# A graph-attention and graph-convolution kernel with a planned step order: a new plan with bends per stage, seven early x tiles in y's ring, and four row tables

## The chip, the cores and the metric

The kernel runs on one core of one Trainium2 chip; the other cores are idle. The metric is the device time of one execution in microseconds (us), the median of several runs. Everything is in float32, except for two scratch tiles.

## The reference, cut to what matters

`x` is (32, 512, 1024): 32 batches b, 512 channels c, 1024 nodes n. `adj` is (512, 512).

```python
# layer 0: attention over nodes, then a projection by adj
h = relu(layernorm(x, axis=-1))              # mean and variance over the 1024 nodes
q = einsum('c,bcn->bn', wq, h)
k = einsum('c,bcn->bn', wk, h)
s = q[:, None, :] + k[:, :, None]            # (b, m, n)
s = where(s > 0, s, 0.01 * s)
att = softmax(s, axis=-1)
agg = einsum('bcn,bmn->bcm', h, att)
x = x + relu(einsum('oc,bcm->bom', adj, agg) + bm[None, :, None])
# layer 1: a projection by adj * adj, elementwise
h = relu(layernorm(x, axis=-1))
x = x + (einsum('bnf,nm->bmf', h, adj * adj) + bias)
```

The score of a pair of nodes depends on q[n] + k[m] alone, and the leaky relu has two branches. For a fixed m the nodes n with q[n] above -k[m] take one branch and all others the second. If the nodes are sorted by q, each m needs one sum over the nodes that come before some position and one over those that come after it. So the attention needs no 1024 x 1024 matrix: it needs the rank of each q, running sums of weighted rows in sorted order from both sides, and for each m a look-up at one position.

## The kernel before

**Work of a batch.** Each batch passes through these stages; names are those of the functions, with their lines in the profile.

- `load` (L223) brings four x tiles of 128 channels x 1024 nodes (512 KB each) by SyncE's queue into a ring `xp` of 7 buffers. `stats`, `norm`, `slopes`, `relu` (L234 to L253) make the layer norm: two statistics instructions a tile and small ones on VectorE, the square root (L244) and the relu (L257) on ScalarE. In layer 0 the relu writes over the x tile.
- `scores` (L265): 32 small matmuls on PE (L269) give q and k as rows; a copy on ScalarE and a round trip over DRAM spread q to all partitions (`qrow`, 512 KB). `columns` (L280) transposes them into columns, two PE instructions (L283). `factors` (L293) makes small vectors on VectorE and ScalarE.
- `value` (L369), eight times: four matmuls each (L372) project 128 nodes by adj; `spread` (L377) copies the result out of PSUM on ScalarE.
- `rank` (L304), eight times on VectorE: how many q are below each node's. `lower` (L323), eight times on ScalarE: how many q lie below -k. `to_rows` (L341), `from_rows` (L353) turn counts into row numbers.
- `scatter` (L382), eight times on GpSimd: an indirect DMA writes the projected rows, with q as a last column, in sorted order into a table in DRAM, `td`. There are three tables, taken in turn by batch. `fetch` (L396) reads them back in sorted order by SyncE's queue, as nine blocks of 126 rows.
- `weights`, `later`, `totals`, `stationary` (L406 to L441) make the exponential weights and masks for the running sums.
- `scan` (L452), nine times on PE: two pairs of matmuls (L455) make the running sums of a block, upward in one half of the partitions, downward in the other. `sums` (L461) follows each scan on ScalarE: it copies the last row of either half into the next block (L465, L466), and then the whole result (L468, L469), which goes to the table by two DMAs. So a scan needs the two row copies of the scan before.
- `gather` (L474), eight times on GpSimd: an indirect DMA fetches for each m the two sums and the row at its position. `excess` and `divide` (L483, L490) make the three factors of the softmax; `weigh` (L500, ScalarE) and `combine` (L504, VectorE, two per 128 nodes) add the three rows by them.
- `turn` (L510), eight times: four transposes on PE (L513) bring 512 nodes x 128 channels back to channel-major form; VectorE adds the relu to the residual (L515), which is x again, brought by `reload` (L229) into a ring `yp` of 7 buffers, since the relu wrote over the first copy.
- Layer 1: the same layer norm on y (the relu writes into a ring of four h tiles), `lift` (L262) adds the bias on VectorE, `propagate` (L517), eight times four matmuls (L520), and `finish` (L526) on VectorE, after which the row of tiles goes out.

**Order of the work.** The order is written out by a plan, not by loops. `PLAN` gives each stage a time for each of its pieces, in us from the batch's start. Batch b starts at b x T, with T = 79.96 (L541). `plan` (L534) hands each piece to `at` (L212), which adds the batch's start and, at the two ends of the program, a bend: `LAST` (last three batches) subtracts a curve of the time in the batch, `FIRST_SHIFT` (first five) adds one. All steps of all batches are then sorted by this time (L566) and emitted in that order; each engine and each queue works through its own instructions in the order of emission. So the times only sort. An engine that reaches an instruction early waits for it, and all that stands behind it on that engine waits too.

A batch of the plan spans some 470 us from its first load to its last finish, so about six batches are in progress at a time: in one period PE does scores, columns and values of batch b, scans of b - 1, turns and propagates of two earlier ones.

**Buffers.** PSUM has eight banks in one ring, used by all PE stages. The tile pools set how far stages may run ahead: `v` (8), fetched blocks (5 of three), sums (2), one gathered tile `G` of eight times 128 rows, small tiles mostly 2, `B` 4, `idg` and `arg` 3. Only one x tile of the program, the fourth of batch 1, is loaded into y's ring (L224). Before the first batch, ScalarE's queue writes four pads into each of the three tables (L189, L190), and PE transposes adj into `wmT` (L192).

Of the kernel before, what the change touches and what calls it, by code (L numbers as in the profile page):

```python
# [24 lines left out]
FAR = -1.0e30  # L25
PLAN = {
    "columns": (5.64,),
    "combine": (
        219.19, 223.04, 210.22, 211.36, 209.63, 210.28, 206.38, 209.6, 225.53,
        228.03, 220.14, 223.34, 225.03, 228.74, 208.88, 211.99,  # L30
    ),
    "divide": (201.44,),
    "excess": (197.53,),
    "factors": (34.87,),
    "fetch": (74.37,),
    "finish": (276.66, 282.71, 287, 301.14, 329.23, 329.75, 319.26, 338.77),
    "from_rows": (70.69,),
    "gather": (166.9, 167.4, 174.29, 175.46, 169.28, 190.2, 170.94, 177.02),
    "later": (84.78,),
    "lift": (257.62, 269.93, 271.07, 272.69),  # L40
    "load": (-128.41, -79.79, -90.39, -54.69),
    "lower": (22.54, 28.23, 27.44, 32.99, 8.04, 17.98, 32.02, 49.72),
    "norm0": (-13.33,),
    "norm1": (246.23,),
    "propagate": (267.02, 272.05, 280.31, 288.2, 304.83, 309.75, 312.6, 314.28),
    "rank": (13.66, 14.97, 27.68, 11.26, 36.34, 41.76, 32.23, 38.44),
    "reload": (211.38, 199.1, 198.01, 219.5),
    "relu0": (-9.09, -8.28, -8.01, -5.63),
    "relu1": (255.11, 255.75, 257.61, 257.81),
    "scan": (90.8, 98.9, 110.43, 116.3, 124.4, 137.24, 146.6, 154.57, 156.26),  # L50
    "scatter": (42.7, 37.63, 33.89, 33.08, 60.84, 49.95, 55.02, 49.29),
    "scores": (3.58,),
    "slopes0": (-13.06,),
    "slopes1": (249.1,),
    "spread": (28.19, 22.49, 20.23, 15.13, 33.75, 48.49, 42.32, 30.04),
    "stationary": (87.74, 100.59, 124.44),
    "stats0": (-88.94, -73.62, -80.02, -31.03),
    "stats1": (236.05, 245.64, 244.58, 238.48),
    "sums": (91.04, 103.93, 115.73, 121.32, 128.67, 145.61, 149.72, 155.13, 157.36),
    "to_rows": (29.48, 45.73),  # L60
    "totals": (89.71,),
    "turn": (230.81, 230.13, 230.45, 232.2, 233.84, 234.71, 233.3, 233.76),
    "value": (6.29, 12.68, 8.15, 4.57, 19.9, 20.34, 17.49, 19.32),
    "weigh": (212.94, 205.72, 204.24, 202.28, 221.56, 216.76, 220.58, 203.48),
    "weights": (84.77,),
}
LAST = (0.94, 0.36, 0.02,)
LAST_KNOTS = (60, 95, 130, 150, 215, 250, 275, 300, 345, 400)
LAST_GAIN = (0, 1.2, 5.7, 20.4, 20.4, 46.5, 53, 74.2, 87.6, 87.6)
FIRST_KNOTS = (-60, 60, 150, 250, 350)  # L70
FIRST_SHIFT = (
    (1.7, -1.4, -0.5, -1.8, -0.5),
    (-1.2, -1.1, -0.4, 0.7, -0.3),
    (-1.7, -1.1, -0.5, 5.2, -0.3),
    (-1.6, -1.2, 3.8, -1.4, -1),
    (1.8, 0.9, 1.3, 0.6, 0.5),
)
# [4 lines left out]
def kernel(  # L82
# [99 lines left out]
    tds = [dr.tile([6 * NB * HP, W], F32, name=f"td_{i}") for i in range(3)]  # L182
# [23 lines left out]
    def bend(knots, values, t):  # L206
        t = min(max(t, knots[0]), knots[-1])
        for a, b, u, v in zip(knots, knots[1:], values, values[1:]):
            if t <= b:
                return u + (t - a) * (v - u) / (b - a)  # L210

    def at(s, t, f, *args):  # L212
        time = s.t0 + t
        if B - 1 - s.b < len(LAST):
            time -= LAST[B - 1 - s.b] * bend(LAST_KNOTS, LAST_GAIN, t)
        if s.b < len(FIRST_SHIFT):
            time += bend(FIRST_KNOTS, FIRST_SHIFT[s.b], t)
        steps.append((time, len(steps), f, args))
# [378 lines left out]
```

## Time and profile before

| | us |
|---|---|
| median of 3 runs | 2414.36 (2412.83 to 2418.43) |
| the profiled execution | 2416.79 |
| its span, from first to last instruction | 2415.1 |
| busy PE in the first 240 us | 191.4 |
| busy PE from 240 to 2240 (2000 us) | 1998.1 |
| busy PE from 2240 to the end (175.1 us) | 154.0 |

The profile is of one execution. Busy time is what the instructions of an engine cover; PE is TensorE's matmuls, DVE VectorE, ACT ScalarE, POOL GpSimd, SP SyncE, and a "q" behind the name is that engine's queue of DMA issues. A group's row gives the line, the engine, the operation, what it writes and reads, and how often. In a timeline each row is a start, a duration, and the instructions run together; brackets show the idle time of the engine just before and what ended it. The chain of waits follows the work that ended last back in time: at each step to what released it, or to the instruction before it on its engine. PE's ends are modelled, so a PE that is shown busy may also be waiting inside an instruction: a matmul that takes longer than its kind usually does is a sign of that. PEclk is the granted clock as a share of the full one.

### The profile page before, as it was taken

The numbers are of one execution on the slowest core, as the hardware profiler recorded it, in microseconds if no ns is written. First come the engines' busy times: TensorE is split into PE (matmuls) and PEld (weight loads), VectorE is DVE, ScalarE is ACT, GpSimd is POOL, SyncE is SP. The second block draws the span as 40 slices with busy tenths as digits, with TensorE's granted clock in tenths as the row PEclk, the third lists the DMA queues.
The fourth block names the chain that finished last, engine by engine and source line by source line (L and its number), as shares of the span: only waits on it lengthen the run. The fifth ranks groups of instructions, "written<-read, shape, count | busy, mean of one in ns | idle before, by whom it ended". The sixth has DMA issues, their size and how long they took to land.

```text
span 2415.1 us, 28224 instructions
## 1 busy us (share of the span) xinstructions
PE 2343.5 (97%) x7632; PEld 986.1 (41%) x7632; DVE 1932.3 (80%) x5012; ACT 1591.2 (66%) x2879; POOL 704.7 (29%) x973
## 2 busy tenths in 40 slices
PE   6889999999999999999999999999999999999898
PEld 2233444443444443444443444443444444444333
DVE  6568787888788888787888888888888888887766
ACT  3667667777676677676777676677666677666541
POOL 2233232233232223232233232223232223232310
PEclk8889999999999999999999999999999999999999
DMA  4698988898898898898898898898898898898772
GB/s 157 164 286 284 279 289 260 268 298 284 275 289 265 255 295 281 273 291 259 253 299 284 278 290 263 254 293 287 273 281 273 251 293 289 273 284 256 237 284 99
DMA packets 206522, 642.87 MB, mean 266 GB/s; under 512 B 29030, under 2 KB 29158, under 8 KB 206364
## 3 DMA queue, kind: packets, MB, share of 16 engines
q1 hardware_dynamic: 146704, 370.65, 54.6%
q0 software_dynamic: 57344, 268.99, 29.3%
q10 hardware_dynamic: 2316, 1.43, 0.3%
q8 instruction: 62, 1.02, 0.2%
q14 instruction: 96, 0.79, 0.1%
HBM read 429.94 MB, written 211.02 MB: 265 GB/s over the span
## 4 chain that ended last, share of the span: by engine, by line
PE 92%; ACT 2%; DMA 2%; DVE 1%; issue 1%; POOL 0%; SPq 0%; ACTq 0%; POOLq 0%; DVEq 0%
PE pv L372 37%; PE pg L520 35%; PE sc L455 13%; PE tr L513 4%; PE pq L269 2%; DMA vs<-td 1%; ACT vs L465 1%; DMA g<-td,idg 1%; ACT x L257 1%; ACT g L502 0%; DVE y L515 0%; DMA td<-pad 0%; PE pd L434 0%; PE pr L283 0%; DMA bm_sb<-in_L_gnn_bm_dram 0%
## 5 line engine op out<-in xcount | busy, mean ns | idle before, releaser
L520 PE MATMUL pg<-h,wsq 128*128 128x512 f32 x2048 | 937.1, 602 | 0.8 <-ACT h L257 0.8
L372 PE MATMUL pv<-wmT,x 128*128 128x512 f32 x2048 | 912.0, 599 | 0.0
L520 PEld LDWEIGHTS pg<-h,wsq 128*128 128x128 f32 x2048 | 373.7, 191 | 515.0 <-issue 476.1
L372 PEld LDWEIGHTS pv<-wmT,x 128*128 128x128 f32 x2048 | 380.8, 191 | 494.8 <-issue 450.7
L477 POOL DMA_INDIRECT g<-td,idg x256 | 246.2, 962 | 800.1 <-DVE qk L288 204.0
L385 POOL DMA_INDIRECT td<-v,idx x256 | 286.7, 1120 | 571.2 <-ACT g L502 186.5
L465 ACT COPY vs<-sc 1x512 f32<-1x512 f32 x256 | 145.7, 569 | 418.1 <-PE sc L455 417.8
L325 ACT ACTIVATE junk<-qrow,qk 128x1024 bf16<-128x1024 f32 x256 | 294.6, 1151 | 141.9 <-DMA qrow<-qd 140.9
L455 PE MATMUL sc<-vs,sm 128*64 128x512 f32 x1152 | 344.0, 631 | 29.7 <-ACT vs L465 20.3
L506 DVE SCALAR_TENSOR_TENSOR g<-g,cf 128x512 f32<-128x512 f32 x512 | 350.0, 747 | 24.8 <-ACT g L502 24.5
L515 DVE SCALAR_TENSOR_TENSOR y<-tr,nbm,y 128x512 f32<-128x512 f32 x256 | 178.8, 744 | 109.2 <-PE tr L513 109.2
L528 DVE SCALAR_TENSOR_TENSOR y<-pg,bm_sb,y 128x512 f32<-128x512 f32 x256 | 188.2, 739 | 85.0 <-PE pg L520 85.0
L468 ACT COPY t<-sc 128x512 f32<-128x512 f32 x288 | 168.6, 585 | 32.4 <-PE sc L455 23.4
L314 DVE TENSOR_SCALAR_CACHE_REDUCE junk<-qrow,qk,cnt 128x640 bf16<-128x640 f32 (+6 forms) x224 | 180.5, 806 | 8.2
L309 DVE TENSOR_SCALAR_CACHE_REDUCE junk<-qrow,qk 128x384 bf16<-128x384 f32 (+6 forms) x224 | 165.9, 740 | 9.3 <-DMA qrow<-qd 7.9
L502 ACT ACTIVATE g<-g,cf 128x512 f32<-128x512 f32 x256 | 163.9, 715 | 2.6 <-DVE cf L496 2.6
L239 DVE BATCH_NORM_STATS2 st<-x 128x6 f32<-128x512 f32 x256 | 162.0, 674 | 2.7 <-DMA x<-in_x_dram 2.6
L239 DVE BATCH_NORM_STATS2 st<-y 128x6 f32<-128x512 f32 x256 | 160.6, 669 | 0.0
L455 PEld LDWEIGHTS sc<-vs,sm 128*64 128x64 f32 x1152 | 67.1, 137 | 228.4 <-issue 121.6
L263 DVE TENSOR_TENSOR y<-y,bias_sb 128x1024 f32<-128x1024 f32 x128 | 153.4, 1220 | 4.5 <-ACT h L257 4.5
L466 ACT COPY vs<-sc 1x512 f32<-1x512 f32 x256 | 147.7, 577 | 5.5
L257 ACT ACTIVATE h<-y,nmr,rstd 128x1024 f32<-128x1024 f32 x128 | 149.2, 1237 | 2.9 <-PE pg L520 2.3
(107 smaller groups left out, 1827.8 us busy)
## 6 DMA issues: line engine op xcount, KB each, us to landing
vs<-td SPq DMA_DIRECT2D x192, 384.8 KB
td<-t SPq DMA_DIRECT2D x576, 128.2 KB
x<-in_x_dram SPq DMA_DIRECT2D x128, 512.0 KB
y<-in_x_dram SPq DMA_DIRECT2D x128, 512.0 KB
out_dram<-y SPq DMA_DIRECT2D x128, 512.0 KB
qrow<-qd SPq DMA_DIRECT2D x32, 512.0 KB
td<-v,idx POOLq DMA_INDIRECT x256, 6.6
g<-td,idg POOLq DMA_INDIRECT x256, 10.7
```

Source lines behind the costliest of these rows:

```text
L239: nc.vector.bn_stats(st[:, i, :], s.x[c][:, ts(i, HALF)])
L257: nc.scalar.activation(h, s.x[c], AF.Relu, bias=s.nmr[:, c : c + 1], scale=s.rstd[:, c : c + 1])
L314: nc.vector.tensor_scalar(junk[:, j * P :], s.qrow[:, j * P :], qc, first, ALU.is_lt, ALU.add, accum_out=s.cnt[:, 1, j : j + 1],)
L325: nc.scalar.activation(junk, s.qrow, AF.Sign, bias=s.qk[:, 1, j : j + 1], accum_out=s.sgn[:, j : j + 1])
L372: nc.tensor.matmul(pv, s.h[c][:, ts(j, P)], wmT[:, c, :], start=(c == 0), stop=(c == NC - 1))
L385: i = nc.gpsimd.indirect_dma_start(tds[s.b % 3][:, :], bass.IndirectOffsetOnAxis(ap=s.idx[j // 4][:, j % 4 : j % 4 + 1], axis=0), v[:, :], ...
L455: nc.tensor.matmul(p[ts(k, HP), :], s.sm[i][k], s.vs[h][:, 0:C], start=True, stop=True)
L477: nc.gpsimd.indirect_dma_start(s.g[:, j, :], None, tds[s.b % 3][0 : 3 * NB * HP, :].rearrange("(s k) w -> s (k w)", k=3), bass.IndirectOff ...
L506: nc.vector.scalar_tensor_tensor(r, s.g[:, j, k * W : k * W + C], s.cf[:, k, j : j + 1], r, ALU.mult, ALU.add)
L515: nc.vector.scalar_tensor_tensor(xh, pt, nbm[:, o : o + 1], xh, ALU.max, ALU.add)
L520: nc.tensor.matmul(pg, wsq[:, r, ts(c, P)], s.h[r][:, ts(i, HALF)], start=(r == 0), stop=(r == NC - 1),)
L528: nc.vector.scalar_tensor_tensor(xh, s.pg.pop((c, i)), bm_sb[:, c : c + 1], xh, ALU.add, ALU.add)
```

## The change

1. Seven x tiles, all four of batch 1 and the first three of batch 2, are loaded into y's ring; before it was the fourth of batch 1 alone.
2. Four tables `td` in place of three; each has its four pad writes.
3. `nq` has three buffers in place of two, `B` five for four, `idg` and `arg` four for three.
4. `PLAN` has new times for all stages, and T is 79.84. `turn` is two stages, one for each half of the nodes, with four times each; the eight pieces are the same.
5. The curves for the first and last batches are gone. In their place each stage has a shift and a stretch (about the stage's mean time) for each of the first five batches, `FIRST`, and of the last five, `LAST`, of which the first pair belongs to the last batch.

No instruction of a batch is added or taken away; the order of the steps differs throughout. Cut to the stages that are spoken of below:

```diff
+TABLES = 4
 PLAN = {
-    "columns": (5.64,),
+    "columns": (1.84,),
-    "divide": (201.44,),
-    "excess": (197.53,),
+    "divide": (197.69,),
+    "excess": (192.58,),
-    "finish": (276.66, 282.71, 287, 301.14, 329.23, 329.75, 319.26, 338.77),
+    "finish": (275.07, 275.57, 281.48, 295.03, 317.93, 325.21, 315.57, 329.77),
-    "lower": (22.54, 28.23, 27.44, 32.99, 8.04, 17.98, 32.02, 49.72),
-    "norm0": (-13.33,),
+    "lower": (19.51, 17.67, 17.14, 24.76, 5.02, 13.05, 20.96, 48.33),
+    "norm0": (-19.68,),
-    "propagate": (267.02, 272.05, 280.31, 288.2, 304.83, 309.75, 312.6, 314.28),
-    "rank": (13.66, 14.97, 27.68, 11.26, 36.34, 41.76, 32.23, 38.44),
+    "propagate": (259.13, 265.4, 277.44, 283.36, 299.38, 300.5, 305.97, 309.52),
+    "rank": (10.11, 17.8, 19.14, 5.65, 29.55, 35.11, 29.97, 33.03),
-    "relu0": (-9.09, -8.28, -8.01, -5.63),
-    "relu1": (255.11, 255.75, 257.61, 257.81),
-    "scan": (90.8, 98.9, 110.43, 116.3, 124.4, 137.24, 146.6, 154.57, 156.26),
+    "relu0": (-13.28, -12.83, -12.78, -11.68),
+    "relu1": (248.39, 248.69, 248.95, 251.18),
+    "scan": (86.07, 89.94, 103.3, 112.5, 121.08, 133.74, 140.67, 149.41, 151.56),
-    "scores": (3.58,),
+    "scores": (-3.28,),
-    "sums": (91.04, 103.93, 115.73, 121.32, 128.67, 145.61, 149.72, 155.13, 157.36),
+    "sums": (86.61, 100.16, 109.91, 113.65, 123.33, 138.82, 142.68, 150.09, 152.34),
-    "turn": (230.81, 230.13, 230.45, 232.2, 233.84, 234.71, 233.3, 233.76),
-    "value": (6.29, 12.68, 8.15, 4.57, 19.9, 20.34, 17.49, 19.32),
-    "weigh": (212.94, 205.72, 204.24, 202.28, 221.56, 216.76, 220.58, 203.48),
+    "turn0": (224.81, 225, 224.25, 224.65),
+    "turn1": (229.2, 229.61, 229.06, 228.65),
+    "value": (1.31, 6.43, 2.58, -2.04, 12.64, 17.61, 9.29, 13.53),
+    "weigh": (211.43, 203.12, 199.8, 199.59, 214.55, 207.84, 213.35, 199.85),
...
 }
-LAST = (0.94, 0.36, 0.02,)
-LAST_KNOTS = (60, 95, 130, 150, 215, 250, 275, 300, 345, 400)
-LAST_GAIN = (0, 1.2, 5.7, 20.4, 20.4, 46.5, 53, 74.2, 87.6, 87.6)
-FIRST_KNOTS = (-60, 60, 150, 250, 350)
-FIRST_SHIFT = (
...
-)
+FIRST = {
+    "columns": ((10.25, 0), (-8.88, 0), (-1.28, 0), (-0.35, 0), (-4.55, 0)),
...
+    "norm0": ((-0.28, 0), (-7, 0), (-16.93, 0), (-5.48, 0), (-7.56, 0)),
...
+    "scan": ((-3.08, 0.008), (0.76, 0.008), (0.29, 0.01), (4.39, 0.049), (0.02, 0.004)),
...
+    "value": ((12.84, -0.049), (-4.18, -0.108), (-0.34, -0.035), (-1.68, 0.56), (-0.83, -0.076)),
...
+}
+LAST = {
...
+    "excess": ((-15.23, 0), (-5.2, 0), (-2.78, 0), (5.24, 0), (-2.45, 0)),
+    "finish": ((37.02, -0.24), (-20.28, -0.179), (-0.12, 0.054), (7.26, 0), (7.17, 0.076)),
...
+    "scan": ((-10.15, -0.309), (-4.12, -0.13), (1, -0), (0.78, -0), (-0.72, 0)),
...
+    "sums": ((-11.31, -0.321), (-3.79, -0.122), (0.67, -0.005), (1.54, -0.003), (-0.48, 0)),
...
+}
@@
-    tds = [dr.tile([6 * NB * HP, W], F32, name=f"td_{i}") for i in range(3)]
+    tds = [dr.tile([6 * NB * HP, W], F32, name=f"td_{i}") for i in range(TABLES)]
@@
-    def at(s, t, f, *args):
-        time = s.t0 + t
-        if B - 1 - s.b < len(LAST):
-            time -= LAST[B - 1 - s.b] * bend(LAST_KNOTS, LAST_GAIN, t)
-        if s.b < len(FIRST_SHIFT):
-            time += bend(FIRST_KNOTS, FIRST_SHIFT[s.b], t)
-        steps.append((time, len(steps), f, args))
@@
-        pool, tag = (yp, "y") if (s.b, c) == (1, NC - 1) else (xp, "x")
+        pool, tag = (yp, "y") if NC <= s.b * NC + c < NC + 7 else (xp, "x")
@@
-        s.nq = sp.tile([P, 2], F32, tag="nq", name=f"nq_{s.b}")
+        s.nq = sp.tile([P, 2], F32, tag="nq", name=f"nq_{s.b}", bufs=3)
...
-        s.B = sp.tile([P, NN], F32, tag="B", name=f"B_{s.b}", bufs=4)
+        s.B = sp.tile([P, NN], F32, tag="B", name=f"B_{s.b}", bufs=5)
@@
-        s.idg = sp.tile([P, NN], U32, tag="idg", name=f"idg_{s.b}", bufs=3)
+        s.idg = sp.tile([P, NN], U32, tag="idg", name=f"idg_{s.b}", bufs=4)
...
-        s.arg = sp.tile([P, 2, NN], F32, tag="arg", name=f"arg_{s.b}", bufs=3)
+        s.arg = sp.tile([P, 2, NN], F32, tag="arg", name=f"arg_{s.b}", bufs=4)
@@
+    T = 79.84
+
     def plan(s, f, name, *lead, args=None):
-        for n, t in enumerate(PLAN[name]):
-            at(s, t, f, s, *lead, *(args[n] if args else (n,)))
-
-    T = 79.96
+        times = PLAN[name]
+        mean = sum(times) / len(times)
+        shift, stretch = 0, 0
+        if s.b < len(FIRST[name]):
+            shift, stretch = FIRST[name][s.b]
+        elif B - 1 - s.b < len(LAST[name]):
+            shift, stretch = LAST[name][B - 1 - s.b]
+        for n, t in enumerate(times):
+            t = s.b * T + t + shift + stretch * (t - mean)
+            steps.append((t, len(steps), f, (s, *lead, *(args[n] if args else (n,)))))
@@
-        plan(s, turn, "turn", args=pairs_of(NH, range(NC)))
+        for i in range(NH):
+            plan(s, turn, f"turn{i}", i)
```

The other uses of `tds[s.b % 3]` become `tds[s.b % TABLES]`, and `pairs_of` is named `all_of`.

## The prediction, made before the changed kernel was run

> **What bounds the kernel now.** First the page: busy time by engine, and the granted TensorE clock over the span.
>
> ```profile
> span 2415.1 us, 28224 instructions
> PE 2343.5 (97%) x7632; PEld 986.1 (41%) x7632; DVE 1932.3 (80%) x5012; ACT 1591.2 (66%) x2879; POOL 704.7 (29%) x973
> PEclk8889999999999999999999999999999999999999
> ```
>
> TensorE sets the time, with two soft ends: the first 240 us hold 191 us of busy PE at a reduced clock, the stretch from 2240 on 154 of 175. I price the three parts apart. For the middle I read the busy times of two batches, each from one start of scores on PE to the next: batch 15, and batch 7 (columns: length; busy PE, its weight loads, VectorE, ScalarE, GpSimd; granted clock, DMA share, GB/s).
>
> ```profile
> 1052.54:1124.86 72.32, 72.23 (x240) 30.41 (x239) 60.21 (x157) 49.60 (x90) 21.97 (x30) 1.00 0.86 277
> 474.76:546.28 71.52, 71.52 (x239) 30.17 (x238) 62.85 (x163) 49.72 (x90) 21.84 (x30) 1.00 0.91 281
> ```
>
> The same 36 PE steps, PE busy throughout at full clock, yet 0.80 us apart. In the PE timeline, 22 batches in a row (8 to 29) take 72.32, batch 7 71.52. The chain of waits shows why: the end of batch 15, then that of batch 7.
>
> ```profile
> 1118.13 3.44 PE pg L520 x8
> 1121.57 1.03 PE sc L455 x4
> 1122.60 0.02 issue
> 1122.63 0.58 ACT vs L465
> 1123.21 0.04 issue
> 1123.25 1.67 PE sc L455 x4
> 1124.93 1.86 PE pq L269 x32
> ```
>
> ```profile
> 540.31 1.01 PE sc L455 x4
> 541.32 0.59 PE tr L513 x4
> 541.91 3.44 PE pg L520 x8
> 545.35 1.01 PE sc L455 x4
> 546.35 1.86 PE pq L269 x32
> ```
>
> In batch 15, scan 7 and scan 8 have one turn between them. Scan 8 needs two rows that sums 7 copies on ScalarE (L465, L466; 0.58 each): its first half starts late, and it takes 1.67 instead of 1.01, waiting for the second row. In batch 7 turn 5 and propagate 7 lie between, and both waits are gone: (1123.25 + 1.67) - 1121.57 = 3.35 for scan, turn, scan, against 1.01 + 0.59 + 1.01 = 2.61 and small switches, 0.80 in all by the period.
>
> Last the two ends, in the timelines of ScalarE and PE.
>
> ```profile
> 20.57 0.89 ACTq L189 DMA_DIRECT2D td<-pad  x2
> 21.49 1.28 ACT L244 ACT_TABLE_LOAD   x1 [21.49 <-DMA td<-pad]
> ...
> 2306.04 0.21 ACT L488 ACTIVATE cf<-cf 128x8 f32<-128x8 f32 x1 [5.74 <-DVE cf L487]
> ```
>
> ```profile
> 2306.81 2.30 PE L455 MATMUL sc<-vs,sm 128*64 128x512 f32 x4 [2.77 <-issue]
> 2365.29 5.39 PE L513 MATMUL tr<-ident,g 128*128 128x128 f32 x32 [3.60 <-DVE g L506]
> ```
>
> At the start the first norm stands behind the pad writes on ScalarE's queue. At the end ScalarE sits 5.74 in the excess of batch 30, which waits for the gather; sums 2 of batch 31 is queued behind it, and scan 3 waits 2.77.
>
> **What the Trainium skill says.** "Perfetto Trace Analysis", Identifying the Most-Contended Engine: TensorE's busy share is a poor measure, since matmuls are pipelined. The trace agrees: 72.23 of 72.32 busy hides 0.80 of waiting. Its Optimization Strategy names bubbles that repeat as a sign of missing memory; here one repeats 22 times and the cause is a copy, not a buffer. "TensorE: Matmul & The Clock Gate", Part 1: an idle PE falls back to half clock; the trace agrees (a scan takes 2.57 at 116.27, 1.01 in the middle). The same part says ScalarE and VectorE are strict first-in first-out, as the 5.74 shows.
>
> **The change, part by part.** I sorted both plans by their times and read the order on each engine.
>
> *Middle.* Every batch has the same PE steps. New: the second value stands before columns; turns go 2, 3, 0, 1, 7, 6, 4; and the end is scan 7, turn 5, propagate 7, scan 8: batch 7's order. One turn between scans 7 and 8 remains in batches 6 and 28 only, 22 before (7 to 28). Two turns (scan 8 at 1.32, so 0.3 lost) stand in three early batches before (2, 3, 5), in one after (4). Gain: (22 - 2) x 0.80 + 2 x 0.3 = 16.6. The cover is propagate 7 (3.44) and the turn (0.59) against 1.2 of copies, once ScalarE is free: scan 7 now comes 3.4 us earlier, but the four relus before sums 7 end at 1114.5 and scan 7 would end at 1119.1. Columns 3.5 later: VectorE waits, but the ranks it feeds start after qrow and totals anyway (14.0 us into the batch). T = 79.84 for 79.96 costs nothing: it only sorts.
>
> New queueing: divide now stands behind rank 5 and finish 1, 1.9 + 0.7 = 2.5 us, so it ends near 1095.0 instead of 1092.5. Weigh waits for it, and sums 4 and 5 queue behind weigh on ScalarE. Weigh started at 1096.41, when ScalarE came free: 1.4 to spare. Sums 5's copies end at 1105.9, scan 6 starts at 1106.9: 1.0 more. That covers the 2.5 but for 0.1, so I take 0; it costs something only where divide ends well after 1095.0 (rival below).
>
> *Front.* A fourth table adds four pad writes on ScalarE. Twelve take 13.05 to 23.72, 0.28 to 0.61 each with waits for landings up to 5.01. Four issues are 1.8; lower bound 0 (behind the relus), upper 1.8 + 5.0 = 6.8; I take 2.5, since the norm waits behind them. Seven x tiles in y's ring: SyncE no longer stops at 32 us for a slot until 56.5, so batch 2 is in SBUF early; but VectorE waited for x only 0.17 there, so 0, and up to 1.9 from the qrow of batch 1 no longer queued behind a 512 KB load. Their slots are free again when value of batches 1 and 2 ends, before the reloads at 162 and on. Norm and relu of batch 1 before the last lower (1.35): PE's 5.10 idle before scores 1 shrinks by 3, but the fetch of batch 0 lands at 79.8 as before; what stays is one more value put into that wait, 2.5. The seven bare scans of batch 0, each waiting for sums, stay (102.8 to 125.1). In batch 1 a value of batch 3 fills the wait between scans 7 and 8, and relus run earlier: 3.5 by scores 3, including the 2.5. Front: +2.5 - 3.5 = -1.0, bounds -6 and +5.
>
> *Tail.* Excess 30 moves behind sums 3 of batch 31: 2.77 of waiting and 2.4 of slow clock around scan 3 go (scan 2.30 for 1.01, propagate 4.67 for 3.63), but all eight weighs (5.0) then stand ahead of sums 5, a new wait of 1.5 at scan 6. Scan 8, and with it the last gather, come 3.7 to 4 earlier. From there on the chain is fixed by gather, combine, turn, stats, relu (2332.82 to 2381.76); propagate 5 of batch 30 moves into the 3.60 wait, but two finishes (1.4) now stand before the last slopes. I take -4.0, bounds -8 and +2. The finish 31 pushed late changes no order that matters: nothing follows it but itself.
>
> Spare copies of nq, B, idg, arg: no instruction, 0.
>
> Sum against the profiled execution: 2415.1 - 16.6 - 1.0 - 4.0 = 2393.5 span, 2395 with the 1.7 around it (2416.79). The three runs have a median of 2414.36, 2.4 below that execution, so 2414.4 - 21.6 = 2393.
>
> **Rivals.**
> *The ends gain more than I see* (shifts fitted per stage; 49 us of idle PE in the first 240, 21 at the end): front -6 or beyond and tail -8: about 2380. For: half of the bare scans' time is waiting. Against: the scans of the first two batches still stand bare in the new order.
> *The wait only moves.* PSUM or the copies hold scan 8 elsewhere: propagates 4, 5, 7 keep three banks to the next batch, scan 7 takes its bank 3.4 us earlier, before turns 7, 6, 4 are read. Half of the 0.80 back: 2401. All of it, or the order not realised: 2409 to 2414, no difference.
> *Slower: divide too late.* VectorE is 84% busy at 71.5 (60.2). Of the spare 1.4 + 1.0 = 2.4 the 2.5 has used all; what divide is late beyond 1095.0 is PE time in each of some 20 batches. From 1.1 us on that eats the gain of 21.6, and at 1.5 it costs 30 - 21.6 = 8: 2422. Against: in batch 7 VectorE did 62.9 within 71.52 unharmed.
>
> **How the numbers follow.** Middle gain as worked, ends within their bounds 0.66; ends gain more 0.08; half moved 0.08; no difference 0.06; slower 0.12. I call 0.2% (4.8 us) what a measurement can tell from none. Faster 0.82, same 0.06, slower 0.12. Likeliest 2393, its own range 2384 to 2402 (front and tail bounds, partly opposed). For 8 in 10 I cut the slower tail and the far end of the first rival: 2381 to 2411.
>
> **What would show it.** Right: starts of scores 71.5 apart over batches 8 to 25; in the chain, scan 7, turn, propagate, scan 8 at 1.01 with no copy between; the 5.74 on excess later than sums 3, no 2.77 at scan 3; relu of batch 0 near 26 instead of 23.77. Wrong: a period above 72, with a scan over 1.1 or a propagate over 3.7 that a copy or a finish released; first scores after 30; the first gather of batch 31 well after 2311 (2332.8 - 16.6 - 1 - 4), say at 2317.

## The result, and the profile after

| | before | changed | ratio (95% interval) |
|---|---|---|---|
| first set of runs, 18 each: median us | 2415.31 | 2410.99 (2404.84 to 2416.22) | 0.998 (0.9973 to 0.9988) |
| the profiled execution, first set | 2416.79 | 2408.70 | |
| second set (19 and 5 runs) | 2412.71 | 2400.82 (2393.64 to 2402.81) | 0.9952 (0.9939 to 0.9964) |
| third set (17 and 5 runs) | 2412.45 | 2398.69 (2396.19 to 2402.67) | 0.9944 (0.993 to 0.9957) |

The change makes the kernel a little faster: by 4.3 us in the first set, where 21.6 was forecast, and by 12 and 14 us in two later sets of the same kernel. Two things are to be explained: where the rest of the gain went, and why the changed kernel moves by 12 us from set to set while the kernel before moves by 3. The executions of one set of the changed kernel also lie 6 to 11 us apart, and the profiled one need not be the middle one: in the second and third set it is the fastest of five, 7.2 and 2.5 us below the median. The later sets ran on several chips, and the chip of the first is not on record, so a difference between sets may be one between chips.

The page of the changed kernel, of an execution of the first set:

```profile
span 2406.7 us, 28301 instructions
PE 2330.6 (97%) x7632; PEld 981.1 (41%) x7632; DVE 1930.8 (80%) x5012; ACT 1589.9 (66%) x2873; POOL 687.6 (29%) x973
PEclk9889999999999999999999999999999999999999
```

PE is busy for 12.9 us less (2343.5 before), but the span is only 8.4 shorter: idle PE has grown from 71.6 to 76.1. Waits inside matmuls went, and open waits came. The busy times of period 15 (from scores 15 to scores 16) and of period 27 show both; the columns are those of the prediction:

```profile
1044.87:1116.43 71.56, 71.56 (x240) 30.18 (x238) 59.87 (x157) 49.88 (x90) 20.79 (x30) 1.00 0.88 277
1899.34:1980.92 81.58, 78.92 (x257) 33.03 (x255) 61.51 (x161) 54.50 (x102) 23.95 (x32) 0.98 0.86 260
```

And the chain of waits at the end of period 15, start and length of each piece:

```profile
1110.47 1.01 PE sc L512 x4
1111.48 0.59 PE tr L570 x4
1112.07 3.44 PE pg L577 x8
1115.51 1.01 PE sc L512 x4
1116.51 1.86 PE pq L326 x32
```

Scan 7, one turn, propagate 7, scan 8, both scans at 1.01, and no copy in the chain: the steady part came as forecast. Scores are 71.57 apart in the 17 periods 9 to 25. Period 27 (its 81.58 hold 17 matmuls more than period 15, since scores 27 themselves stand earlier in the new order) has open waits.

For the whole span I set every step on PE beside its usual length: the time from its start to the next step's start, less what the same pair of steps takes in the steady periods of the changed kernel, set so that a steady period loses nothing. What is left over is lost time. Some pairs stand at the two ends only and have no steady length; other choices for them shift the front and the tail of every row alike, by some 3 us, so it is the differences between rows that count. Summed by stretches, up to the last step on PE, in us:

| trace | first scores start | to scores 4 | periods 4-8 | 9-25 | 26-30 | from scores 31 on | sum |
|---|---|---|---|---|---|---|---|
| before, first set | 25.1 | 48.1 | 1.5 | 12.8 | 3.1 | 27.9 | 118.4 |
| changed, first set | 27.2 | 39.1 | 4.9 | 0.0 | 9.9 | 28.6 | 109.7 |
| changed, second set | 27.1 | 37.5 | 2.3 | 0.0 | 6.3 | 21.5 | 94.7 |
| changed, third set | 27.0 | 39.1 | 1.8 | 0.0 | 5.7 | 23.6 | 97.2 |

The difference of the sums, 8.7 for the first two rows, agrees with that of the spans, 8.4. So the 17 steady periods gained their 12.8 and the front 6.9; 3.4 were lost again in periods 4 to 8, 6.8 in periods 26 to 30, and the tail gained nothing in this execution, but 6.4 and 4.3 in the two others. Of the 9.9 in periods 26 to 30, 4.9 are in period 27; periods 26, 28, 29 and 30 lose 0.7 to 2.1 each.

The loss in period 27, on ScalarE's timeline and then PE's (start, length; in brackets the idle time before and what ended it):

```profile
1972.19 0.30 ACT L468 ACTIVATE w<-vs,nq 128x3 f32<-128x3 f32 x1
...
1974.39 0.30 ACT L468 ACTIVATE w<-vs,nq 128x3 f32<-128x3 f32 x1 [1.71 <-DMA vs<-td]
...
1977.41 0.30 ACT L468 ACTIVATE w<-vs,nq 128x3 f32<-128x3 f32 x1 [2.53 <-DMA vs<-td]
...
1977.81 0.56 ACT L522 COPY vs<-sc 1x512 f32<-1x512 f32 x1
```

```profile
1978.42 2.57 PE L512 MATMUL sc<-vs,sm 128*64 128x512 f32 x4 [2.59 <-ACT vs L522]
```

The new bends reach back to batch 27 and set its `weights` 8.67 us earlier. They now stand on ScalarE ahead of sums 7 of batch 26 and wait there, piece by piece, for the fetch of batch 27. The row copies queue behind them, and scan 8 of batch 26 behind the copies: 2.59 open, and 1.49 more inside the scan (2.50 to the next step, for 1.01).

There are stalls in periods 5 and 8 too:

```profile
385.01 1.97 PE L570 MATMUL tr<-ident,g 128*128 128x128 f32 x16 [1.85 <-DVE g L563]
```

```profile
556.26 1.53 PE L512 MATMUL sc<-vs,sm 128*64 128x512 f32 x4 [1.22 <-POOL sm L502]
```

In the first a turn waits for combine, which is late since the gather of batch 3 took 11.15 us to land in the chain of waits. In the second a stationary waits behind a gather on GpSimd's queue (2.07 us idle before that gather; what held it, the profile doesn't show). The second stall is absent in the other two traces (period 8 back at 71.57), the first smaller by 0.8 and 1.3.

### The profile page after: what moved, and what is told of

It is laid out like the page before. It is cut to its first block, busy times and chain, and to the rows that moved or that the text cites. A ratio compares the mean times of both kernels' runs of the same rounds, so it can differ in the third digit from the quotient of the medians.

```text
span 2406.7 us, 28301 instructions
## 1 busy us (share of the span) xinstructions
PE 2330.6 (97%) x7632; PEld 981.1 (41%) x7632; DVE 1930.8 (80%) x5012; ACT 1589.9 (66%) x2873; POOL 687.6 (29%) x973
## 3 DMA queue, kind: packets, MB, share of 16 engines
q1 hardware_dynamic: 146704, 370.65, 54.5%
## 4 chain that ended last, share of the span: by engine, by line
PE 82%; DMA 5%; DVE 5%; ACT 3%; issue 2%; POOL 1%; SPq 1%; ACTq 0%; POOLq 0%; DVEq 0%
PE pg L577 33%; PE pv L429 31%; PE sc L512 11%; PE tr L570 4%; PE pq L326 2%; DMA vs<-td 1%; DMA td<-v,idx 1%; DMA qd<-qr 1%; DVE junk L371 1%; DVE st L296 1%; DVE g L563 1%; DMA qrow<-qd 1%; DVE junk L366 1%; ACT g L559 1%; POOL td L442 1%
## 5 line engine op out<-in xcount | busy, mean ns | idle before, releaser
L442 POOL DMA_INDIRECT td<-v,idx x256 | 272.1, 1063 | 572.6 <-ACT vs L523 208.2
L522 ACT COPY vs<-sc 1x512 f32<-1x512 f32 x256 | 146.0, 570 | 388.4 <-PE sc L512 375.9
L512 PE MATMUL sc<-vs,sm 128*64 128x512 f32 x1152 | 332.2, 629 | 28.3 <-ACT vs L522 17.2
L559 ACT ACTIVATE g<-g,cf 128x512 f32<-128x512 f32 x256 | 169.6, 717 | 3.1 <-DVE cf L553 2.9
L436 ACT COPY v<-pv 128x512 f32<-128x512 f32 x256 | 144.3, 578 | 20.1 <-PE pv L429 13.8
L314 ACT ACTIVATE x<-x,nmr,rstd 128x1024 f32<-128x1024 f32 x128 | 148.5, 1232 | 9.6 <-DVE nmr L307 9.6
```

The costliest lines, as they stand in the source:

```text
L442: i = nc.gpsimd.indirect_dma_start(tds[s.b % TABLES][:, :], bass.IndirectOffsetOnAxis(ap=s.idx[j // 4][:, j % 4 : j % 4 + 1], axis=0), v[: ...
L512: nc.tensor.matmul(p[ts(k, HP), :], s.sm[i][k], s.vs[h][:, 0:C], start=True, stop=True)
L559: nc.scalar.mul(r, r, s.cf[:, 0, j : j + 1])
```

## The experiments

Three theories. **A**: the order on PE gives 0.75 to 0.80 a steady batch, and what was lost at the ends was put there by the bends, step by step, and can be taken back. **B**: the new order, its end above all, hangs on when transfers land; the losses vary from execution to execution. **The wait only moves** (a rival of the prediction): the 0.8 was slack, and any tighter order pays it back elsewhere.

### The order at the end of a batch, alone and undone

e2, in the kernel before:

```diff
-    "propagate": (267.02, 272.05, 280.31, 288.2, 304.83, 309.75, 312.6, 314.28),
+    "propagate": (267.02, 272.05, 280.31, 288.2, 304.83, 309.75, 312.6, 314.9),
```

> The kernel before with one number changed: propagate 7 at 314.9 in place of 314.28, so that PE does scan 7, turn 5, propagate 7, scan 8 in every batch. Theory A: 0.75 to 0.80 less in each of the 22 batches 7 to 28, nothing lost at the ends: 2415.3 - 17 = 2398, faster than the changed kernel. Theory B: the 0.8 was slack that kept late transfers from stopping PE; single stalls come in its place and the time is near that of the changed kernel, 2408 to 2413.

Measured: 2396.16 (before 2412.71; ratio 0.993, 0.9917 to 0.9943), 16.6 us less, by one number. Its busy times in period 15, and its chain there:

```profile
1044.49:1116.06 71.57, 71.57 (x241) 30.18 (x239) 59.81 (x157) 49.62 (x90) 21.95 (x30) 1.00 0.88 282
```

```profile
1110.09 1.01 PE sc L455 x4
1111.10 0.59 PE tr L513 x4
1111.68 3.43 PE pg L520 x8
1115.12 1.01 PE sc L455 x4
```

All periods from 8 to 30 but one (71.70) take 71.57. Nothing came in the wait's place.

e3, in the changed kernel:

```diff
-    "propagate": (259.13, 265.4, 277.44, 283.36, 299.38, 300.5, 305.97, 309.52),
+    "propagate": (259.13, 265.4, 277.44, 283.36, 299.38, 300.5, 305.97, 309.02),
```

> The changed kernel with propagate 7 at 309.02 in place of 309.52: scan 7, turn 5, scan 8 again, as before the change. Theory A: 0.75 more in each of some 20 batches, 2411 + 15 = 2426. Theory B: less than that, 2411 to 2418, since the stalls of the tight order go away.

Measured: 2413.98, 13.2 above the changed kernel of the same set (2400.82). The time itself lies in B's range, since the changed kernel took 2400.82 and not 2411 here; the difference is near A's 15. The copy is back in the chain, and scan 8 at 1.68:

```profile
1117.64 1.03 PE sc L512 x4
1118.67 0.02 issue
1118.69 0.58 ACT vs L522
1119.28 0.04 issue
1119.32 1.68 PE sc L512 x4
```

So the place of propagate 7 is worth 16.6 us in the old plan and 13.2 in the new one, and the rival of the moving wait falls for the steady periods. In the second set e2, with the old start, the old bends and three tables, is 4.7 us faster than the whole change: all that the change does besides this order cost more there than it brought.

### The same kernel again

No edit. 

> The changed kernel once more, unaltered, for a second trace. Theory A (fixed losses: each stall is put there by the order, above all the weights of batch 27 in front of sums 7 of batch 26): the same stalls at the same places, 4 us at scan 8 of batch 26, a period of 71.57 in batches 9 to 25; time 2408 to 2412. Theory B (tight plan: transfers that land late by chance stop a queue now here, now there): the period is 71.57 in most batches, but the single stalls near batches 5, 8 and 26 are gone or stand elsewhere.

> The changed kernel once more, for a third trace, since its first set of runs and the second differ by 10 us. Theory B (the end hangs on when the fetch of batch 31 and the gather of batch 30 land): the lost time after the last scores is anywhere between 21 and 28 us, and follows the time from the issue of that fetch to its last landing (16.5 us in the first trace, 13.4 in the second); the rest of the span is equal within 2 us but for batches 5, 8 and 27. Rival: the whole span is stretched on one chip, then steady periods differ too.

Measured: 2400.82 and 2398.69 (table above), 7 to 11 us below what A had said for e1. Of theory A the stall at scan 8 of batch 26 is there in all three traces (lost time in period 27 over a steady one: 4.9, 2.5 and 2.5); of theory B, period 8 is whole again in both, and the tail moves between 21.5 and 28.6. Both are in part right. The rival of e11 (everything stretched) is out: the steady periods agree to 0.01 us.

What moves the tail is the fetch of batch 31. From scores 31 to PE's totals of batch 31 the three traces agree to 0.01 us step by step; there the first is 4.30 behind the second. SyncE's queue issues the fetch at 2261.88 in the first trace and at 2252.67 in the second; the landing of its thirds is seen on ScalarE's timeline, where the weights wait for them. The first trace, then the second:

```profile
2268.57 0.30 ACT L468 ACTIVATE w<-vs,nq 128x3 f32<-128x3 f32 x1 [8.40 <-DMA vs<-td]
...
2272.27 0.30 ACT L468 ACTIVATE w<-vs,nq 128x3 f32<-128x3 f32 x1 [3.21 <-DMA vs<-td]
...
2278.42 0.30 ACT L468 ACTIVATE w<-vs,nq 128x3 f32<-128x3 f32 x1 [5.67 <-DMA vs<-td]
```

```profile
2258.80 0.30 ACT L468 ACTIVATE w<-vs,nq 128x3 f32<-128x3 f32 x1 [7.85 <-DMA vs<-td]
...
2262.41 0.30 ACT L468 ACTIVATE w<-vs,nq 128x3 f32<-128x3 f32 x1 [3.12 <-DMA vs<-td]
...
2266.09 0.30 ACT L468 ACTIVATE w<-vs,nq 128x3 f32<-128x3 f32 x1 [3.20 <-DMA vs<-td]
```

From issue to the last landing it is 16.5 us in the first, 13.4 in the second; 13.2 in the third, and 13.4 in the kernel before and in e2. PE's totals of batch 31 wait for it, 5.57 idle in the first and 1.28 in the second. The busy times over these two stretches (last two columns DMA share, GB/s):

```profile
2261.88:2278.42 16.54, 11.32 (x39) 5.66 (x37) 6.84 (x13) 0.98 (x4) 4.78 (x5) 0.99 0.99 236
2252.67:2266.09 13.42, 12.50 (x42) 6.12 (x40) 7.28 (x14) 0.98 (x4) 4.78 (x5) 1.00 0.98 215
```

The DMA engines are full in both. What differs is the second queue: the packets, MB and share of the engines' time of SyncE's queue (q1) and of GpSimd's (q0) in the same two stretches, the first trace, then the second:

```profile
q1 hardware_dynamic: 1332, 2.49, 72.4%
q0 software_dynamic: 243, 1.40, 26.4%
```

```profile
q1 hardware_dynamic: 1334, 2.49, 87.5%
q0 software_dynamic: 63, 0.39, 10.5%
```

SyncE's queue moves the same 2.49 MB in both, of which the fetch is 2.31. GpSimd's packets are the gathers of batch 30, issued while the fetch is in flight. The first of them on GpSimd's timeline, in the first trace and in the second:

```profile
2266.61 0.98 POOL L534 DMA_INDIRECT g<-td,idg  x1 [17.51 <-DMA vs<-td]
```

```profile
2258.57 0.98 POOL L534 DMA_INDIRECT g<-td,idg  x1 [18.10 <-DMA vs<-td]
```

It comes 4.73 us after the fetch is issued in the first trace and 5.90 after it in the second. In the first its packets begin at 2273.26, when 238 KB of SyncE's queue are still to come, and these take 5.16 us: 46 KB a us, for 197 up to the second landing. In the second they begin at 2264.51, with 47 KB to come. The same can be read in the other traces. In all eleven with the new bends of the last batches (e3, e4 and e12 alter one time each) the first gather of batch 30 starts at the same place, while the fetch moves (us after the start of scores 31):

| traces | fetch issued | first gather | fetch takes |
|---|---|---|---|
| second, third, e3, e4, e7, e12, e13 | 60.3 to 61.2 | 66.7 | 13.2 to 13.9 |
| e9 | 61.2 | 66.7 | 15.3 |
| first | 61.9 | 66.7 | 16.5 |
| e14 (added transfers, below) | 62.3 | 66.7 | 16.8 |
| e18 (twice as many) | 64.1 | 66.7 | 20.4 |
| seven with the end of the kernel before | 63.4 to 64.7 | 71.1 | 13.1 to 13.7 |

So the new end leaves less time between the two, and a fetch that is issued a little later runs into the gathers. No run here moves the gathers alone.

The 4.30 are not the whole 7.1 between these two tails. Another 2.3 come in the five steps behind the wait, where the granted clock is 0.50 to 0.62 in the first trace and 1.00 in the second. In the third it is 0.50 to 0.68 after a wait of 1.11 only, which is why it loses 2.1 more than the second with the same fetch; what sets the clock there stays open. Averaged over the executions of a set it is 0.986, 0.988 and 0.990, the slowest set first; as the steady periods agree, it can act at the ends alone, and its part isn't separated from that of the waits.

Over the whole span the same packets of SyncE's queue took longer in the first set; the rows give packets, MB, and the share of 16 engines' span:

```profile
q1 hardware_dynamic: 146704, 370.65, 54.5%
```

```profile
q1 hardware_dynamic: 146704, 370.65, 53.9%
```

54.5% of 2406.7 is 1312 us, 53.9% of 2391.6 is 1289: 1.7% more (third set 1290).

### Added transfers

e14 to e17 add the same copies to four kernels, e18 and e19 twice as many. The edit, for the single dose:

```diff
+    spare = [dr.tile([QUAD, N], F32, name=f"spare_{i}") for i in range(8)]
...
+    def more(b, i):
+        nc.sync.dma_start(spare[(4 * b + i) % 8], x[b % B, ts(i, QUAD), :])
...
+    for b in range(1, B + 3):
+        for i in range(4):
+            steps.append((b * T + 20 * i, len(steps), more, (b, i)))
     steps.sort(key=lambda e: e[:2])
```

> The changed kernel with 512 KB a batch copied from x to a spare place in DRAM besides, in four pieces, by SyncE's queue, 2 to 3% more bytes than it moves anyway; the work is otherwise the same. The slower set of runs of the changed kernel had 1.7% more transfer time on that queue than the faster ones. Theory B (its end and its fifth, eighth and 27th period hang on landings): 6 to 12 us more than the 2399 to 2401 of the faster sets, with the additional loss in those periods and the tail. Rival: under 3 us more.

> The same copies in the kernel before with propagate 7 moved. Theory B: its steady order is as tight as that of the changed kernel but its ends are not bent as far, so it loses less: 0 to 4 us more than 2396. Rival (any tight order suffers): as much as the changed kernel, 6 to 12.

> The same copies in the mixed version, which has the new start and the old end. Theory B: what the changed kernel loses besides this one is due to the new end; 1 to 5 us more than 2390.5. Rival: as much as the changed kernel.

> The same copies in the kernel before. Theory B: 0 to 4 us more than 2412.5, as in the set of runs in which it took 2415.3 while the changed kernel took 2411. Rival: as much as the changed kernel loses.

> The changed kernel with twice the added copies, 1 MB a batch in eight pieces; the work is otherwise the same. With 512 KB it lost 4.4 to 6.5 us in the median, the mixed version 5.6. Theory B in its weaker form (the changed kernel's end is the more sensitive one): 10 us or more above 2400, at least 4 more than the mixed version loses; late landings show in the fetch of batch 31 (16 us and over) and in the fifth period. Rival (all tight orders lose alike): both lose the same within 2 us.

> The mixed version with 1 MB of added copies a batch. Theory B: 2390.5 + 6 to 9; the end keeps 28 to 30 us of lost time and the periods 18 to 30 keep 71.57. Rival: as much as the changed kernel loses, 10 or more.

| median us | no copies | 512 KB a batch | 1 MB a batch |
|---|---|---|---|
| changed | 2400.8, 2398.7 | 2405.15 | 2413.89 |
| mixed (e10, below) | 2390.5 | 2396.16 | 2398.98 |
| before, propagate 7 moved | 2396.2 | 2400.39 | |
| before | 2412.5, 2412.7 | 2416.56 | |

With the single dose theory B fell short: the changed kernel lost 4.3 to 6.5 us, not 6 to 12, the mixed version 5.7, the others 4 (3.3 for the kernel before beside its own set, 2413.24). In the versions with the old end some of this is no wait at all: their last copies stand behind the last output, and from PE's last step to the end of the span it is 6.4 to 6.5 us, and 8.3 with the double dose, for 4.8 without copies. In the changed kernel it stays at 4.5. The double dose parts them: the changed kernel loses 13 to 15 and is then no faster than the kernel before without copies (2413.83 in that set; ratio 1.0, 0.9992 to 1.0008), the mixed version 8.5, of which 3.5 are such copies. The two with the double dose ran in one set, on a chip on which neither ran without copies. In the trace of the changed kernel with the double dose the fetch of batch 31, issued at 2264.52, takes 20.4 us:

```profile
2284.90 0.30 ACT L472 ACTIVATE w<-vs,nq 128x3 f32<-128x3 f32 x1 [8.60 <-DMA vs<-td]
```

and 36.4 us are lost from scores 31 on; with the single dose 16.8 and 30.2 (both traces are among the slowest of their sets). The copies put the fetch later, 62.3 and 64.1 us after scores 31, and the gathers stay at 66.7. Over the five traces of the changed order with four tables and no edit of the plan the two go together: 13.2, 13.4, 16.5, 16.8, 20.4 us for the fetch, 23.6, 21.5, 28.6, 30.2, 36.4 lost. In the mixed version the fetch keeps 13.5 and 13.1 us under both doses and its tail 29.3 and 28.6. So more transfers do make this end longer, and the old end hardly. That the first set's 2411 has this cause is supported by its trace, but not shown: why its fetch is issued 1.2 us later and its transfers took 1.7% longer stays open.

### The bends of the end

e4, in the changed kernel:

```diff
-    "weights": ((-3.88, 0), (-2.01, 0), (-1.64, 0), (4.37, 0), (-8.67, 0)),
+    "weights": ((-3.88, 0), (-2.01, 0), (-1.64, 0), (4.37, 0), (-7.0, 0)),
```

> The changed kernel with one bend altered: the shift of weights for the fifth batch from the end is -7.0 in place of -8.67, so that ScalarE does sums 7 of batch 26 before the weights of batch 27. Theory A: scan 8 of batch 26 no longer waits 4.1 us, the period of batch 27 falls by that, 2411 - 4 = 2407. Theory B: the lateness of the fetch shows up one step later (totals or the first scan of batch 27) and the time stays at 2411.

Measured: 2400.94, against 2400.82 of the changed kernel in the same set. Scan 8 of batch 26 is free, as A said, and PE waits for the same fetch one step later, as B said, since the bends also put totals of batch 27 ahead of the first value of batch 28:

```profile
1978.33 0.39 PE L491 MATMUL pd<-w,mask_a 128*64 128x9 f32 x2 [2.26 <-ACT w L468]
```

The values after it then run slowly (16 matmuls in 9.85 us, for 7.06 elsewhere), and periods 26 to 30 lose 9.1, more than in any unaltered trace but the first. So B's reading held; neither 2407 nor 2411 did, since the whole set is faster.

e5 takes the bends of batches 27 and 28 away:

```diff
-        elif B - 1 - s.b < len(LAST[name]):
+        elif B - 1 - s.b < 3:
```

> The changed kernel with its bends for the last three batches alone; batches 27 and 28 run unbent, as 26 does. Theory A (the bends of batches 27 and 28 put steps in front of others that then wait for the fetch: weights 27 before sums 7, totals 27 before the first value of batch 28): the periods of batches 26 to 29 fall to 71.57, 3 to 6 us less than the changed kernel on the same chip; a ratio to the kernel before of 0.993 to 0.994 where the changed kernel had 0.9952. Theory B (late transfers, wherever the steps stand): no gain, 0.995 or above, with a wait in batches 29 to 31 in its place.

Measured: 2402.01, ratio 0.9962 (0.9949 to 0.9976). Periods 26 and 27 are at 71.57, so the bends were what put the stalls there; but 30.3 us are lost from scores 31 on, for 21.5 to 28.6, with the fetch at 13.7 us. What batches 27 and 28 lose, the tail had been getting.

e6 puts the curve of the kernel before in place of all the new bends of the end (the old `bend`, `LAST`, `LAST_KNOTS` and `LAST_GAIN`, under other names):

```diff
-            shift, stretch = LAST[name][B - 1 - s.b]
+            gain = GAINS[B - 1 - s.b]
+            times = [t - gain * bend(GAIN_KNOTS, GAIN, t) for t in times]
```

> The changed kernel with the curve of the kernel before for the last three batches in place of the new bends. Theory A: the tail takes as long as before the change (27.5 us of lost time after the last scores), and the front and the middle keep their gains, 5 + 16: 0.991 of the kernel before, better than the changed kernel, whose new end would then be worth less than nothing. If the new bends of the last three batches do shorten the tail by the 6 us that the second trace of the changed kernel shows, this one is 4 to 6 us slower than the kernel with the last three bends alone.

Measured: 2411.03, ratio 0.9996 (0.9987 to 1.0004). Periods 26 to 30 are whole, and the tail loses 43.0: the curve doesn't suit the new plan. PE waits for the fetch of batch 31 and then for combine:

```profile
2272.68 0.38 PE L494 MATMUL pd<-w,mask_a 128*64 128x9 f32 x2 [10.04 <-ACT w L471]
...
2353.78 2.82 PE L573 MATMUL tr<-ident,g 128*128 128x128 f32 x12 [9.06 <-DVE g L566]
```

The fetch takes 17.1 us; the gathers of batch 30 start 4.25 after it. The tail was expected at 27.5, or some 5 above that of e5; it is 12.7 above it. A bend has to be made for its plan.

e12, the exponential of batch 30's excess ahead of sums 2 of batch 31 again:

```diff
-    "excess": ((-15.23, 0), (-5.2, 0), (-2.78, 0), (5.24, 0), (-2.45, 0)),
+    "excess": ((-15.23, 0), (-9.9, 0), (-2.78, 0), (5.24, 0), (-2.45, 0)),
```

> The changed kernel with the exponential of batch 30's excess moved back in front of sums 2 of batch 31 on ScalarE, as it stood before the change. My step of the prediction: scan 3 of batch 31 waits again for a copy that is queued behind the exponential, and the end comes 2.8 to 4 us later than in the changed kernel. Rival: the exponential is late because it stands behind sums that wait for the fetch of batch 31; ahead of them it lets divide, weigh and combine of batch 30 start sooner, and the end is the same or earlier.

Measured: 2399.40, beside 2398.69 in the same set. ScalarE waits there again:

```profile
2288.03 0.21 ACT L545 ACTIVATE cf<-cf 128x8 f32<-128x8 f32 x1 [3.97 <-DVE cf L544]
```

but PE's scan behind it waits 0.84, for 2.77 before the change, and the medians differ by 0.7 us only, not by 2.8 to 4: the end is about the same, as the rival allowed (its reason is not shown), and the place of the exponential decides nothing by itself.

### The front

e7, in the changed kernel:

```diff
-TABLES = 4
+TABLES = 3
```

> The changed kernel with three tables in place of four, and so four pad writes less ahead of the first norm. My step: the first scores start at 25.1 in place of 27.2, and 2 us of that reach the scores of batch 3; nothing else changes, 2 us less than the changed kernel. Rival: the fetch of batch 0 or its scans are what the front waits for and the 2 us are gone by scores of batch 3; no difference. If a table is needed again before it is free, a stall in every period shows it, and the time is longer.

Measured: 2397.34, ratio 0.9935 (0.9922 to 0.9949), for 0.9952 and 0.9944 with four. The first norm on ScalarE's timeline, behind the pads, with four tables and with three:

```profile
23.92 1.28 ACT L301 ACT_TABLE_LOAD   x1 [23.92 <-DMA td<-pad]
```

```profile
20.34 1.28 ACT L301 ACT_TABLE_LOAD   x1 [20.34 <-DMA td<-pad]
```

Scores start at 27.25 with four and 23.91 with three: the pads are 3.3 us there, and 3 to 4 are left at scores 4 (27.2 + 39.1, 27.1 + 37.5 and 27.0 + 39.1 lost up to there with four, 23.9 + 37.9 with three). No later period asks for the fourth table.

e9 and e13 put the curves of the kernel before in place of `FIRST`; e13 has besides

```diff
-        pool, tag = (yp, "y") if NC <= s.b * NC + c < NC + 7 else (xp, "x")
+        pool, tag = (yp, "y") if (s.b, c) == (1, NC - 1) else (xp, "x")
```

> The changed kernel with the curves of the kernel before for the first five batches, everything else as changed (four tables, seven x tiles in y's ring). Theory A (the new bends make the front's gain): scores of batch 3 start at 186 to 187 in place of 184.5 and the stalls in the periods of batches 5 to 8 are other ones; 2 to 6 us more than the changed kernel. Rival (the x tiles make it, since batch 2 is in SBUF early): scores of batch 3 at 184.5 as in the changed kernel.

> The changed kernel with the curves of the kernel before for its first five batches and only the one x tile in y's ring. Beside the run with these curves and seven x tiles it tells what the tiles do by themselves. My step: nothing, within 2 us, first scores at 28, scores of batch 3 at 191.5. Rival: with the loads of batch 2 waiting for slots of x's ring, the row of q of batch 1 is queued behind them on SyncE and scores of batch 3 come later by 2 us or more.

Measured: 2412.34 with seven tiles, 2412.19 with one. Scores 3 start at 191.5 and 189.7 (184.4 in the third trace of the changed kernel). The tiles do nothing by themselves under these curves, as the step had it; the new bends of the start gain 12 to 14 us over the old ones in the new plan, at least twice what theory A had for e9. A single x tile with the new bends wasn't tried.

### A mixed version

e10: three tables, the first 18 batches as changed, from batch 18 on the plan of e2 (`OLD_PLAN`) and the old curve at the end.

```diff
+        if s.b >= SWITCH:
+            times = OLD_PLAN[name]
+            if B - 1 - s.b < len(GAINS):
+                gain = GAINS[B - 1 - s.b]
+                times = [t - gain * bend(GAIN_KNOTS, GAIN, t) for t in times]
+            times = [t - LEAD for t in times]
```

with SWITCH = 18 and LEAD = 5.0.

> A version meant to beat both kernels: the changed kernel with three tables, its first 18 batches as changed, and from batch 18 on the plan and the end curve of the kernel before with propagate 7 at 314.9, all 5 us earlier in the plan. Theory A (front, middle and end are separate sums): first scores at 24, lost time up to the scores of batch 3 some 37 us (46 before), 0.75 gained in every steady batch to the 30th, the tail 27.5 us as before: 1 + 9 + 17 = 27 less, a ratio of 0.989. Theory B (the stalls of the tight order come by chance): single stalls between batches 18 and 30, 0.993 or above.

Measured: 2390.51, ratio 0.9909 (0.9894 to 0.9924): faster than the kernel before, the change and e2. By stretches it loses 23.9, 38.8, 1.2, -0.1, 0.0 and 27.8, 26.8 less than the trace of the kernel before, as A's sum of 27 had it; between the medians it is 21.9, since that trace is of a slower execution (2416.79) than the median of this set (2412.45). Beside e7, which differs in plan and end from batch 18 on, it is 6.8 us faster in the median, on another chip. The fastest executions are alike, 2390.20 and 2390.55: the new end can cost nothing, but e7's five executions reach 2397.36 where the mixed version's four reach 2392.91.

## Why the prediction was wrong

- **What bounds the kernel, and the 0.80.** Right: 71.57 a period where 71.5 was forecast, and the order alone is worth 16.6 in e2. That this is the middle's sum to the tenth is luck in part: e2 frees 22 periods at 0.75 each (72.32 to 71.57), the sum had 20 at 0.80 and 0.6 for early batches. The missing 0.05 is batch 7's own: it takes 71.53 in e2 too, for 71.57.
- **The gain of the middle, (22 - 2) x 0.80 + 0.6 = 16.6, for the changed kernel.** This is the step that failed. The periods 4 to 30 gained 2.6 (17.4 to 14.8) in the first set, 8.8 and 9.9 in the two later ones. I looked through the new order on PE for one pattern, scan, turn, scan, in every batch, but read ScalarE's order in a steady batch and in the last two only. In the five bent batches at either end other steps stand ahead of the copies or on PE itself, and wait for transfers: weights of batch 27 before sums 7, totals of 27 before a value, a turn of batch 3 behind a late gather. With smaller losses that I haven't traced, periods 26 to 30 cost 6.8 and 4 to 8 cost 3.4 more than before, against 12.8 gained in 9 to 25. The 16.6 was right as a sum over the place of scan 8; for the rest of the order in the bent periods I had taken 0.
- **New queueing, divide at 1095.0.** Right: 42.46 us after the start of its period was worked out, 42.4 measured, and no stall; the rival of a late divide did not come.
- **Front, -1.0 (bounds -6 and +5).** Measured -6.9 up to scores 4, just outside (some -5.7 up to scores 3). The pads were right in kind (2.5 taken, 2.2 between the first two traces, 3.3 by e7). The x tiles were right (0), as far as they were tried, under the old curves. Mis-sized was the order: -3.5 taken, -9.0 measured from the first scores to scores 4 (48.1 to 39.1). On the later sets, beside e2's front (24.9 + 45.5), the whole is -5.8 and -4.3.
- **Tail, -4.0 (bounds -8 and +2).** +0.7 in the first set, -6.4 and -4.3 in the others: inside the bounds, but for another reason. The excess step, worth 2.77 to me, is worth no more than the 0.7 between the medians of e12 and the changed kernel. What decides is the landing of the last fetch: I had taken the chain behind the scans as it was before, and not asked whether the gathers of batch 30, 4.4 us earlier after scores 31 (66.7 for 71.1), would meet that fetch. This is the second term that failed, by 4.7 in the first set.
- **The sum.** 1.0 + 16.6 + 4.0 = 21.6 against 6.9 + 2.6 - 0.7 = 8.8 in the trace. Of the 12.8 between, the middle is 14.0 and the tail 4.7, and the front gave back 5.9. The profiled execution was the fourth fastest of its 18, 2.3 us below their median, and the one before 1.5 above its own; so 4.3 between the medians.
- **The rivals.** Of "the ends gain more than I see" the front came true (-6.9), the tail (-8) did not; "the wait only moves" gives about the right time, but not its mechanism: no bank and no copy held scan 8 in a steady batch.

## What to carry to other kernels

Where a plan bends the order for the first and last iterations, each bent iteration has to be read on every in-order engine as the steady one is: ahead of each step that the bound engine needs, is there one that waits for a transfer? An order that is tighter only by computing steps kept its gain under load (e2: 16.6 us without added copies, 16.2 with them), one that leans on transfers landing on time has a time that varies with them; it should be tried with some transfers added. A transfer that PE waits for should be looked at beside all queues: what another queue starts while it is in flight can hold its last part, as the gathers did here. And one number of a plan may hold most of a change: look for it before tuning all.

## What was not expected of the hardware

The same kernel gave medians of 2411.0, 2400.8 and 2398.7 in three sets of runs, the kernel before 2415.3, 2412.7 and 2412.5; the same 146704 packets of SyncE's queue took 1312, 1289 and 1290 us of the 16 engines' time. And with the DMA engines 98 to 99% busy, the last 238 KB of SyncE's queue in one fetch took 5.16 us once GpSimd's gathers had begun beside it, 46 KB a us for 197 before; a fetch that was issued 1.2 us later (61.95 for 60.77 after the last scores) landed 4.3 later.
